# Weights read from PSUM, member matrices in pieces, pinned row fields and inputs prepared three tiles at a time in a four-layer graph network

## The chip, the cores and the metric

The kernel runs on one core of one Trainium2 chip. The time is device microseconds for one execution. Before the change the median of three runs is 3754.58 us (3746.37 to 3756.95). The engines are called TensorE (PE; its weight loads are shown apart as PEld), VectorE (DVE), ScalarE (ACT), GpSimd (POOL) and SyncE (SP). SP, ACT and POOL also issue DMA transfers. SBUF is the memory of the core that all engines read; PSUM is the small memory that TensorE writes.

## The reference

There are 1875 nodes with 256 values each, and 31875 edges sorted by destination, with 32 attributes, a type (0 to 7) and a weight each. Four layers follow each other; each has a graph part and a feed-forward part, and each part gets the normalised rows and is added to x.

- Layer 0: four rounds of GINE (for each edge relu(x[src] + edge_attr @ eW + eb), summed by destination, then two matrix products), and a feed-forward part on about half of the rows.
- Layer 1: attention over relations. For each edge the row of its source under the weights of its type, a score for each of 8 heads, a softmax over the edges of a destination, and the weighted sum. In short:

```
scores = leaky(h_src·attn_src + h_dst·attn_dst, 0.2)
amax   = max(segment_max(scores, dst), 0)
w      = exp(scores - amax[dst])
out    = segment_sum(h_src * w, dst) / (segment_sum(w, dst) + 1e-12)
```

  Then a feed-forward part of eight experts, one for each row, with a limit on rows.
- Layer 2: two GCN products (h = x @ W, then a sum over neighbours with dinv[src] * weight * dinv[dst], plus a bias; relu between them, softmax behind), then eight experts, two for each row, weighted.
- Layer 3: one GCN product with relu, added to its input, then sixteen experts, two for each row, and a final LayerNorm with gamma and beta.

## The kernel before

Rows are held in 15 tiles (NT) of 128 nodes, the last of 83; x stays in SBUF. A scheduler takes the program in its written order and may move instructions ahead on each engine; `later` keeps an instruction in program order. A tile pool gives each name a number of buffers, and a new use waits until the last reader of the old buffer is done. SP and ACT issue plain loads in the order of their own instructions; POOL issues indirect gathers and scatters.

**Attention** (fast_layer1_gnn, L835 and behind it). All rows under all eight relations, 264 values each (256 and the 8 source scores), lie in a table in DRAM. The edges of a destination tile are cut into 18 columns of 128 edges (12 for the last tile). For tile t `attention_edges` issues 18 gathers (L1122) into g, builds s16 (L873: 1 where the edge's destination is the column's node, 128 x 18 x 128) and sT (L879: its transpose, from a row of destinations), and computes the destination's score of every edge (L888, L890, L896). `attention_scores` forms the scores (L918) and runs a maximum within each column; `attention_weights` turns this into the maximum of each node (L950 through s16), brings it back to the edges (mk, L962 through sT), and stores exp of the score minus it into g's last 8 columns (L967). Three multiplications of six columns each (L970) weight the gathered rows in place. `attention_sums` adds up the edges by TensorE (L983) and divides (L985 to L988). The written order for each t is edges(t), scores(t-1), sums(t-2), weights(t-1). g has four buffers, s16 three, sT two, mk and ptop one each.

**GCN** (fast_gcn). Normalised tiles are transposed (L497) and copied to xT by ACT (L498), multiplied by W (L1019) and scaled into h (L1021); then for each tile 15 products with its adjacency tile (L1025) are summed and finished (L1028, L1030). The 15 adjacency tiles, 128 x 1920 float32 each, are loaded by SP (L997). In layers 2 and 3 all 15 tiles are normalised ahead, three at a time (`moments` with the square root on ACT, L1173, and L1205).

**Routing and experts.** Behind each group of finished tiles `route` picks two experts for each row, writes row, gate (L1772) and token number (L1773) into one of two row buffers, and scatters the rows to their slots (L1128). The two row buffers lie in one tile: in layer 2 in `first`, in layer 3 in a tile named rowbufs, of 2 * CH * 2 * (D + 2) values (CH is 3). `few_experts` then loads weights and slots for each block of rows, computes, and scatters the results to f_outs (L1128). When all are written (`complete`, a memset on POOL), the two outputs of each row are loaded (sum, L1912; even tiles on SP, odd ones on ACT, 15 buffers), added on POOL (L1913) and into x or y on DVE (L1914).

**The end** (layer3_ffn). Three tiles at a time: moments, L2009 and L2011, and the store.

Of the kernel before, what the change touches and what calls it, by code (L numbers as in the profile page):

```python
# [40 lines left out]
P = 128  # L41
N = 1875
NT = 15
# [56 lines left out]
class Net:  # L100
# [333 lines left out]
    def fast(self):  # L434
        with self.tc.tile_pool(name="win", bufs=1) as self.wpool:
# [5 lines left out]
            with self.tc.tile_pool(name="k2", bufs=1) as sb:  # L441
                r = self.router2(sb)
                self.fast_layer2_gnn(r)
                self.layer2_ffn(r)
            with self.tc.tile_pool(name="k3", bufs=1) as sb:
                r = self.router3(sb)
                self.fast_layer3_gnn(r)
                self.layer3_ffn(r)

    def slow(self):  # L450
# [9 lines left out]
        with self.tc.tile_pool(name="k2", bufs=1) as sb:  # L460
            r = self.router2(sb)
            self.route_all(self.route2, r)
            self.layer2_ffn(r)
        self.layer3_gnn()
# [397 lines left out]
    def attention_edges(self, t, table, ad3, hot, pools):  # L862
# [10 lines left out]
        nc.vector.tensor_tensor(s16, self.iota[:, None, :].to_broadcast([P, n, P]),  # L873
                                self.wdst[:, c0:c0 + n, None].to_broadcast([P, n, P]), ALU.is_equal)
# [4 lines left out]
        nc.vector.tensor_scalar(sT.rearrange("p j e -> p (j e)"), row, self.token[:, t:t + 1], None,  # L879
                                op0=ALU.is_equal)  # L880
# [61 lines left out]
    def attention_weights(self, a, pools):  # L942
# [24 lines left out]
        nc.scalar.activation(g[:, :, D:], sc, AF.Exp)  # L967
        for j0 in range(0, n, 6):
            v = g[:, j0:j0 + 6, :D].rearrange("p j (h d) -> p j h d", d=HD)
            nc.vector.tensor_tensor(v, v, g[:, j0:j0 + 6, D:, None].to_broadcast([P, 6, H, HD]),  # L970
                                    ALU.mult)
# [32 lines left out]
    def fast_gcn(self, pre, x, adj, wb, done):  # L1004
# [3 lines left out]
        with ExitStack() as ctx:  # L1008
# [5 lines left out]
            for t in range(NT):  # L1014
                xT = sb.tile([P, KD, P], F32, name="xT")
# [18 lines left out]
    def fast_layer2_gnn(self, r):  # L1034
        nc, tc, a = self.nc, self.tc, self.a
        with tc.tile_pool(name="q2a", bufs=1) as ap, tc.tile_pool(
            name="q2", bufs=1
        ) as one, tc.tile_pool(name="q2r", bufs=1) as rp:
# [5 lines left out]
            with tc.tile_pool(name="q2n", bufs=3) as sb:  # L1044
                self.layernorm_by(first, self.x, sb, CH)
# [16 lines left out]
            self.fast_gcn("d0", first, adj, ws[0], relu)  # L1062
            self.fast_gcn("d1", y, adj, ws[1], softmax)

    def fast_layer3_gnn(self, r):
        nc, tc, a = self.nc, self.tc, self.a
        with tc.tile_pool(name="q3a", bufs=1) as ap, tc.tile_pool(
            name="q3", bufs=1
        ) as one, tc.tile_pool(name="q3r", bufs=1) as rp:
# [3 lines left out]
            self.rows_in(r, one.tile([P, 1, ROWS], F32, name="rowbufs"))  # L1073
            with tc.tile_pool(name="q3n", bufs=3) as sb:
                for t in range(0, NT, CH):
                    self.layernorm(xl[:, t:t + CH, :], self.x[:, t:t + CH, :], sb)
                    for u in range(t, t + CH):
                        nc.gpsimd.tensor_tensor(self.x[:, u, :], self.x[:, u, :], xl[:, u, :],
                                                ALU.add)
# [7 lines left out]
            self.fast_gcn("d2", xl, adj, ws, add)  # L1087
# [119 lines left out]

    def layernorm_by(self, out, x, sb, n):

        for t in range(0, NT, n):  # L1210
            self.layernorm(out[:, t:t + n, :], x[:, t:t + n, :], sb)
# [507 lines left out]
    def route(self, r, ts, x, fill, weigh, sb, ps):  # L1719
# [37 lines left out]
        for i in range(2):  # L1757
# [10 lines left out]
            else:  # L1768
# [3 lines left out]
            nc.vector.tensor_copy(rows[:, :, i, D:D + 1], gates[i][:, :, None])  # L1772
            nc.vector.tensor_scalar(rows[:, :, i, D + 1:], self.token[:, sl, None], float(i * NP),  # L1773
                                    None, op0=ALU.add)
# [58 lines left out]
    def few_experts(self, pre, r, act, f, acc, w1n, w2n, b2n, affine):  # L1833
# [7 lines left out]
        with ExitStack() as ctx:  # L1841
# [63 lines left out]
            done = self.complete(g)  # L1905
            with tc.tile_pool(name=f"{pre}s", bufs=2) as sb:
                for t in range(NT):
                    n = min(P, N - t * P)
                    s = sb.tile([P, 2, D], F32, name="sum", bufs=NT)
                    v = r.outs[0:2 * NP, :].rearrange("(i n) d -> n i d", i=2)  # L1910
# [369 lines left out]
```

## Time and profile before

| | us |
|---|---|
| median of 3 runs | 3754.58 |
| profiled execution | 3750.91 |
| its span (first to last instruction) | 3749.1 |
| layer 0, GINE | about 100 to 1545 |
| layer-1 attention | 1860 to 2296 |
| layer-2 inputs | 2571 to 2610 |
| layer-2 GCN products | 2610 to 2860 |
| layer-2 experts | 2895 to 3235 |
| layer-3 inputs | 3235 to 3297 |
| layer-3 GCN product | 3297 to 3432 |
| layer-3 experts | 3432 to 3700 |
| end | 3700 to 3749 |

The granted TensorE clock is 0.888 on average. Over the span PE is busy 2895.0 us (77%), DVE 1891.3 (50%), POOL 1588.9 (42%), ACT 937.2 (25%).

A timeline row gives the start and the length of an instruction in us, its engine, its line in the kernel, what it writes and reads (out<-in), its shapes, and in brackets how long its engine stood idle before it and what ended that. SPq, ACTq and POOLq rows are the issuing of a DMA, not its transfer. A group row gives the count behind x, the busy time, the mean in ns of one, and the idle time before them.

### The profile page before, as it was taken

How to read it: one execution, taken by the hardware profiler on the slowest of the kernel's cores; microseconds unless marked ns; L12 is line 12 of the kernel's file. 1: busy time of each engine (PE TensorE's matmuls, PEld its weight loads, DVE VectorE, ACT ScalarE, POOL GpSimd, SP SyncE). 2: the span in 40 equal slices, each digit the busy share in tenths (PEclk: the TensorE clock that was granted, in tenths of full speed). 3: DMA queues.
4: the chain of work that ended last, by engine and by line, in shares of the span. 5: the costliest groups of instructions: out<-in, count | busy, mean ns of one | idle time of the engine just before them, and what ended most of it. 6: DMA issues, size and time to landing. Idle time of an engine off the chain costs nothing. (4 is left out here: it accounts for less than half of the span.)

```text
span 3749.1 us, 43548 instructions
## 1 busy us (share of the span) xinstructions
PE 2895.0 (77%) x14049; PEld 2402.2 (64%) x14049; DVE 1891.3 (50%) x5527; ACT 937.2 (25%) x2026; POOL 1588.9 (42%) x1603
## 2 busy tenths in 40 slices
PE   3878789979997999668735555884986999596994
PEld 2667678768776877446524444663875888475773
DVE  5566577756675676683246663016145111445334
ACT  1333233323332333213311111110133222122221
POOL 2777477757775777100177771001011111313222
PEclk9999899989998999789967666896987999798997
DMA  5434656655664453113444430524002555513664
GB/s 147 124 110 129 198 152 202 184 155 162 185 186 136 132 122 113 48 38 96 144 120 142 143 106 29 164 86 173 1 18 80 193 179 177 197 71 96 206 202 136
DMA packets 330707, 495.36 MB, mean 132 GB/s; under 512 B 79601, under 2 KB 258724, under 8 KB 328676
## 3 DMA queue, kind: packets, MB, share of 16 engines
q1 hardware_dynamic: 250804, 286.21, 24.3%
q0 software_dynamic: 72672, 199.68, 18.1%
q10 hardware_dynamic: 6992, 6.58, 0.5%
q8 instruction: 113, 1.85, 0.2%
q14 instruction: 126, 1.03, 0.1%
HBM read 369.90 MB, written 122.43 MB: 131 GB/s over the span
## 5 line engine op out<-in xcount | busy, mean ns | idle before, releaser
L1122 POOL DMA_INDIRECT g<-qt,w_src x1056 | 1036.8, 982 | 431.0 <-issue 351.7
L623 PE MATMUL acc<-m,s 128*128 128x256 f32 (+1 forms) x2112 | 560.6, 389 | 15.5 <-ACT m L610 15.5
L594 PE MATMUL pe<-ew,w_attr 128*128 128x256 f32 x1888 | 509.1, 395 | 69.2 <-DVE g L609 68.6
L609 DVE TENSOR_TENSOR g<-g,pe 128x512 f32<-128x512 f32 x528 | 360.2, 682 | 398.1 <-DMA g<-qt,w_src 341.0
L610 ACT ACTIVATE m<-g 128x512 f32<-128x512 f32 x528 | 332.7, 631 | 795.3 <-DVE g L609 610.0
L1122 POOL DMA_INDIRECT g<-rq_h,w_tsrc x264 | 304.6, 1154 | 390.8 <-PE pz L888 311.0
L594 PEld LDWEIGHTS pe<-ew,w_attr 128*128 128x128 f32 x1888 | 364.2, 197 | 153.4 <-DVE g L609 88.0
L623 PEld LDWEIGHTS acc<-m,s 128*128 128x128 f32 x2112 | 404.8, 196 | 65.0 <-ACT m L610 17.0
L1893 PE MATMUL hid<-xeT,w 128*128 128x256 f32 x1184 | 271.6, 386 | 23.5 <-DVE xeT L1888 23.5
L1899 PE MATMUL out<-w,hidT 128*128 128x256 f32 x1184 | 264.0, 379 | 0.0
L1893 PEld LDWEIGHTS hid<-xeT,w 128*128 128x128 f32 x1184 | 221.1, 192 | 62.6 <-DVE xeT L1888 30.8
L1895 ACT ACTIVATE hidT<-hid,cols 128x256 f32<-128x256 f32 x296 | 138.5, 474 | 450.3 <-PE hid L1893 434.0
L1899 PEld LDWEIGHTS out<-w,hidT 128*128 128x128 f32 x1184 | 225.0, 190 | 30.6
L601 DVE TENSOR_TENSOR s<-iota,w_dst 128x256 f32<-128x256 f32 x528 | 219.3, 416 | 0.0
L401 PE MATMUL padj<-col,row 128*128 128x240 f32 x720 | 207.3, 383 | 15.1 <-DVE col L374 13.0
L1902 DVE TENSOR_TENSOR ye<-out,b 128x256 f32<-128x256 f32 x104 | 44.1, 424 | 313.3 <-PE out L1899 313.3
L1128 POOL DMA_INDIRECT f_outs<-ye,f2place x44 | 42.7, 971 | 299.8 <-DVE ye L1903 276.2
L401 PEld LDWEIGHTS padj<-col,row 128*128 128x128 f32 x720 | 141.7, 199 | 37.2 <-DVE col L374 9.9
L1128 POOL DMA_INDIRECT f_slots<-first,slot x30 | 29.6, 988 | 286.4 <-issue 206.7
L374 DVE TENSOR_SCALAR col<-wide,g_col,g_wt 128x240 f32<-128x240 f32 x360 | 146.4, 407 | 0.0
L983 PE MATMUL acc<-g,s 128*128 128x264 f32 x528 | 139.4, 422 | 5.5 <-issue 3.0
L1128 POOL DMA_INDIRECT f_outs<-ye,f3place x60 | 57.7, 961 | 201.6 <-DVE ye L1903 198.8
(425 smaller groups left out, 4330.0 us busy)
## 6 DMA issues: line engine op xcount, KB each, us to landing
f_slots<-zeros SPq DMA_DIRECT2D x45, 1032.0 KB
w<-in_L_ffn_W SPq DMA_DIRECT2D x44, 1024.0 KB
adj<-adj SPq DMA_DIRECT2D x45, 960.0 KB
w<-in_L_ffn_w SPq DMA_DIRECT2D x60, 512.0 KB
w<-in_L_ffn_w SPq DMA_DIRECT2D x18, 1024.0 KB
g<-qt,w_src POOLq DMA_INDIRECT x1056
dstrow<-lin SPq DMA_DIRECT2D x14, 1152.0 KB
rq_h<-hr SPq DMA_DIRECT2D x8, 1980.0 KB
```

Source lines behind the costliest of these rows:

```text
L374: pin(nc.vector.tensor_scalar(col, self.wide, self.gcol[:, i:i + 1], self.gwt[:, i:i + 1], op0=ALU.is_equal, op1=ALU.mult))
L401: pin(nc.tensor.matmul(pa[:, u // GT, :], row, col, start=u % GT == 0, stop=u % GT == GT - 1))
L594: pin(nc.tensor.matmul(pes[q][:, v, :], at[:, v, :], self.ew[:, i, :], start=True, stop=True))
L601: pin(nc.vector.tensor_tensor(ss[q], self.iota[:, None, :].to_broadcast([P, 2, P]), self.wdst[:, c:c + 2, None].to_broadcast([P, 2, P]), A ...
L609: pin(nc.vector.tensor_tensor(g, g, pes.pop(q), ALU.add))
L610: pin(nc.scalar.activation(m[:, :, :D], g, AF.Relu))
L623: pin(nc.tensor.matmul(accs[t], s[:, v, :], m[:, v, :], start=k == v == 0, stop=end and v == 1))
L983: nc.tensor.matmul(acc, s[:, j, :], g[:, j, :], start=j == 0, stop=j == n - 1)
L1122: self.nc.gpsimd.indirect_dma_start(out=out, out_offset=None, in_=table, in_offset=bass.IndirectOffsetOnAxis(ap=at, axis=0))
L1893: nc.tensor.matmul(p1, w1[:, kc, m * P:(m + 1) * P], xT[:, kc, :], start=kc == 0, stop=kc == KD - 1)
L1895: nc.scalar.activation(hT[:, m, :], p1, act, bias=v[:, m:m + 1])
L1899: nc.tensor.matmul(p2, hT[:, m, i * P:(i + 1) * P], w2[:, m, :], start=m == 0, stop=m == fc - 1)
```

## The change

Five things change together.

1. In the attention ACT copies the softmax weights into PSUM (into mk, whose values are used by then), and the multiplications read them from there; s16 and sT are each written in pieces of six columns.
2. `fast_gcn` takes a function `ready` that prepares three tiles; it is called for the first six tiles ahead of the first transpose, and then three tiles ahead. Layer 2 gives the LayerNorm.
3. `few_experts` no longer loads and adds the outputs. `outputs_of` does so for one tile. For layer 2's experts it is called in layer 3's `ready`, which takes six pieces of rowbufs in place of the 15 sum buffers; the adjacency loads come ahead of it in the program.
4. In the last stage `outputs_of` is called for three tiles ahead of their LayerNorm, with 9 sum buffers.
5. The writes of gate and token number keep their place in program order.

```diff
@@ fast
+            r2 = r
             with self.tc.tile_pool(name="k3", bufs=1) as sb:
                 r = self.router3(sb)
-                self.fast_layer3_gnn(r)
+                self.fast_layer3_gnn(r, r2)
@@ attention_edges
-        nc.vector.tensor_tensor(s16, self.iota[:, None, :].to_broadcast([P, n, P]),
-                                self.wdst[:, c0:c0 + n, None].to_broadcast([P, n, P]), ALU.is_equal)
+        for j in range(0, n, 6):
+            nc.vector.tensor_tensor(s16[:, j:j + 6], self.iota[:, None, :].to_broadcast([P, 6, P]),
+                                    self.wdst[:, c0 + j:c0 + j + 6, None].to_broadcast([P, 6, P]),
+                                    ALU.is_equal)
...
-        nc.vector.tensor_scalar(sT.rearrange("p j e -> p (j e)"), row, self.token[:, t:t + 1], None,
-                                op0=ALU.is_equal)
+        for j in range(0, n, 6):
+            nc.vector.tensor_scalar(sT[:, j:j + 6].rearrange("p j e -> p (j e)"),
+                                    row[:, j * P:(j + 6) * P], self.token[:, t:t + 1], None,
+                                    op0=ALU.is_equal)
@@ attention_weights
+        weights = mk[:, :, 0, :]
+        nc.scalar.copy(weights, g[:, :, D:])
         for j0 in range(0, n, 6):
             v = g[:, j0:j0 + 6, :D].rearrange("p j (h d) -> p j h d", d=HD)
-            nc.vector.tensor_tensor(v, v, g[:, j0:j0 + 6, D:, None].to_broadcast([P, 6, H, HD]),
-                                    ALU.mult)
+            nc.vector.tensor_tensor(v, v, weights[:, j0:j0 + 6, :, None]
+                                    .to_broadcast([P, 6, H, HD]), ALU.mult)
@@ fast_gcn
             for t in range(NT):
+                if ready and t % CH == 0:
+                    for u in (0, CH) if t == 0 else (t + CH,):
+                        if u < NT:
+                            ready(range(u, u + CH))
                 xT = sb.tile([P, KD, P], F32, name="xT")
@@ fast_layer2_gnn
-            with tc.tile_pool(name="q2n", bufs=3) as sb:
-                self.layernorm_by(first, self.x, sb, CH)
+            def ready(ts):
+                sl = slice(ts[0], ts[-1] + 1)
+                self.layernorm(first[:, sl, :], self.x[:, sl, :], np2)
...
-            self.fast_gcn("d0", first, adj, ws[0], relu)
+            self.fast_gcn("d0", first, adj, ws[0], relu, ready)
@@ fast_layer3_gnn
-            self.rows_in(r, one.tile([P, 1, ROWS], F32, name="rowbufs"))
-            with tc.tile_pool(name="q3n", bufs=3) as sb:
-                for t in range(0, NT, CH):
-                    self.layernorm(xl[:, t:t + CH, :], self.x[:, t:t + CH, :], sb)
-                    for u in range(t, t + CH):
-                        nc.gpsimd.tensor_tensor(self.x[:, u, :], self.x[:, u, :], xl[:, u, :],
-                                                ALU.add)
+            buf = one.tile([P, 1, ROWS], F32, name="rowbufs")
+            self.rows_in(r, buf)
+            room = [buf[:, 0, i * 2 * D:(i + 1) * 2 * D].rearrange("p (i d) -> p i d", i=2)
+                    for i in range(ROWS // (2 * D))]
+
+            def ready(ts):
+                for t in ts:
+                    self.outputs_of(r2, t, room[t % len(room)], self.x)
+                sl = slice(ts[0], ts[-1] + 1)
+                self.layernorm(xl[:, sl, :], self.x[:, sl, :], np3)
+                for t in ts:
+                    nc.gpsimd.tensor_tensor(self.x[:, t, :], self.x[:, t, :], xl[:, t, :], ALU.add)
...
-            self.fast_gcn("d2", xl, adj, ws, add)
+            self.fast_gcn("d2", xl, adj, ws, add, ready)
@@ route
-            nc.vector.tensor_copy(rows[:, :, i, D:D + 1], gates[i][:, :, None])
-            nc.vector.tensor_scalar(rows[:, :, i, D + 1:], self.token[:, sl, None], float(i * NP),
-                                    None, op0=ALU.add)
+            self.later(nc.vector.tensor_copy(rows[:, :, i, D:D + 1], gates[i][:, :, None]))
+            self.later(nc.vector.tensor_scalar(rows[:, :, i, D + 1:], self.token[:, sl, None],
+                                               float(i * NP), None, op0=ALU.add))
@@ few_experts
-            done = self.complete(g)
-            with tc.tile_pool(name=f"{pre}s", bufs=2) as sb:
-                for t in range(NT):
-                    n = min(P, N - t * P)
-                    s = sb.tile([P, 2, D], F32, name="sum", bufs=NT)
-                    v = r.outs[0:2 * NP, :].rearrange("(i n) d -> n i d", i=2)
-                    queue = nc.scalar if t % 2 else nc.sync
-                    self.behind(queue.dma_start(s[:n], v[t * P:t * P + n]), done)
-                    nc.gpsimd.tensor_tensor(s[:n, 0, :], s[:n, 0, :], s[:n, 1, :], ALU.add)
-                    nc.vector.tensor_tensor(acc[:n, t, :], acc[:n, t, :], s[:n, 0, :], ALU.add)
+            r.done = self.complete(g)
+
+    def outputs_of(self, r, t, s, acc):
+
+        nc = self.nc
+        n = min(P, N - t * P)
+        v = r.outs[0:2 * NP, :].rearrange("(i n) d -> n i d", i=2)
+        queue = nc.scalar if t % 2 else nc.sync
+        self.behind(queue.dma_start(s[:n], v[t * P:t * P + n]), r.done)
+        nc.gpsimd.tensor_tensor(s[:n, 0, :], s[:n, 0, :], s[:n, 1, :], ALU.add)
+        nc.vector.tensor_tensor(acc[:n, t, :], acc[:n, t, :], s[:n, 0, :], ALU.add)
@@ layer3_ffn
             for t in range(0, NT, CH):
                 ts = slice(t, t + CH)
+                for u in range(t, t + CH):
+                    self.outputs_of(r, u, sb.tile([P, 2, D], F32, name="sum", bufs=9), y)
```

More of the change, by code (lines that the diff above doesn't have):

```diff
@@ L463, in slow @@
             self.layer2_ffn(r)
+            with self.tc.tile_pool(name="k2s", bufs=4) as sp:
+                for t in range(NT):
+                    self.outputs_of(r, t, sp.tile([P, 2, D], F32, name="sum"), self.x)
         self.layer3_gnn()
@@ L1002, in gcn_weights, with fast_gcn @@
         return self.weight(sb, w, f"gw{i}"), self.vector_row(sb, b, f"gb{i}")
-    def fast_gcn(self, pre, x, adj, wb, done):
+    def fast_gcn(self, pre, x, adj, wb, done, ready=None):
         nc, tc = self.nc, self.tc
@@ L1037, in fast_layer2_gnn @@
             name="q2", bufs=1
-        ) as one, tc.tile_pool(name="q2r", bufs=1) as rp:
+        ) as one, tc.tile_pool(name="q2r", bufs=1) as rp, tc.tile_pool(name="q2n", bufs=3) as np2:
             ws = [self.gcn_weights(one, i, a[f"L2_gnn_W{i}"], a[f"L2_gnn_b{i}"]) for i in (1, 2)]
@@ L1060, in softmax, with fast_layer3_gnn @@
                 self.route_behind(self.route2, r, t, rp, ps)
-            self.fast_gcn("d0", first, adj, ws[0], relu)
+            self.fast_gcn("d0", first, adj, ws[0], relu, ready)
             self.fast_gcn("d1", y, adj, ws[1], softmax)
-    def fast_layer3_gnn(self, r):
+    def fast_layer3_gnn(self, r, r2):
         nc, tc, a = self.nc, self.tc, self.a
@@ L1068, in fast_layer3_gnn @@
             name="q3", bufs=1
-        ) as one, tc.tile_pool(name="q3r", bufs=1) as rp:
+        ) as one, tc.tile_pool(name="q3r", bufs=1) as rp, tc.tile_pool(name="q3n", bufs=2) as np3:
             ws = self.gcn_weights(one, 3, a["L3_gnn_W"], a["L3_gnn_b"])
@@ L1206, in layernorm @@
                                          op0=ALU.subtract, op1=ALU.mult)
-    def layernorm_by(self, out, x, sb, n):
-        for t in range(0, NT, n):
-            self.layernorm(out[:, t:t + n, :], x[:, t:t + n, :], sb)
     def affine(self, x, g, b):
@@ L1831, in routed, with few_experts @@
         return filled
-    def few_experts(self, pre, r, act, f, acc, w1n, w2n, b2n, affine):
+    def few_experts(self, pre, r, act, f, w1n, w2n, b2n, affine):
         nc, tc, a = self.nc, self.tc, self.a
@@ L1961, in layer2_ffn @@
     def layer2_ffn(self, r):
-        self.few_experts("e2", r, AF.Gelu, 4 * D, self.x, "L2_ffn_W1", "L2_ffn_W2", "L2_ffn_b2",
-                         True)
+        self.few_experts("e2", r, AF.Gelu, 4 * D, "L2_ffn_W1", "L2_ffn_W2", "L2_ffn_b2", True)
     def router3(self, sb):
@@ L2000, in layer3_ffn @@
                 nc.gpsimd.tensor_tensor(self.x[:, t, :], self.x[:, t, :], bet, ALU.add)
-            self.few_experts("e3", r, AF.Relu, 2 * D, y, "L3_ffn_w1", "L3_ffn_w2", "L3_ffn_b2",
-                             False)
+            self.few_experts("e3", r, AF.Relu, 2 * D, "L3_ffn_w1", "L3_ffn_w2", "L3_ffn_b2", False)
             for t in range(0, NT, CH):
                 ts = slice(t, t + CH)
+                for u in range(t, t + CH):
+                    self.outputs_of(r, u, sb.tile([P, 2, D], F32, name="sum", bufs=9), y)
                 v = y[:, ts, :]
```

## The prediction

> **What bounds the kernel now.** I read the page first. Over the whole span TensorE is busiest (77%), but the change touches stages that other things bound, so I cut the span into stretches, and read each with its groups and its timeline. Time in the first fence is start:end, length, then the busy time of PE, PEld, DVE, ACT and POOL, granted clock, DMA share and GB/s.
>
> ```profile
> 1860.00:2296.00 436.00, 224.15 (x1878) 180.99 (x1878) 260.84 (x472) 68.06 (x176) 300.81 (x261) 0.69 0.40 115
> 2571.00:2610.00 39.00, 29.02 (x130) 23.95 (x131) 18.48 (x73) 6.03 (x19) 0.07 (x1) 0.79 0.92 374
> 3235.00:3297.00 62.00, 24.19 (x113) 19.61 (x114) 36.79 (x105) 7.20 (x21) 23.95 (x32) 0.66 0.78 301
> ```
>
> The attention (first row) is bound by POOL's gathers: busy 301 of 436 us, and between two of them lie only about 0.30 us of "issue". So what counts there is how long one gather takes.
>
> ```profile
> L609 DVE TENSOR_TENSOR g<-g,pe 128x512 f32<-128x512 f32 x528 | 360.2, 682 | 398.1 <-DMA g<-qt,w_src 341.0
> L1122 POOL DMA_INDIRECT g<-rq_h,w_tsrc x264 | 304.6, 1154 | 390.8 <-PE pz L888 311.0
> L970 DVE TENSOR_TENSOR g<-g 128x1536 f32<-128x1536 f32 x44 | 74.7, 1750 | 1.1 <-ACT g L967 1.1
> L873 DVE TENSOR_TENSOR s<-iota,w_dst 128x2304 bf16<-128x2304 f32 (+1 forms) x15 | 37.4, 2496 | 0.0
> L879 DVE TENSOR_SCALAR sT<-dstrow,token 128x2304 bf16<-128x2304 f32 (+1 forms) x15 | 20.9, 1391 | 0.0
> ```
>
> The mean gather is 1154 ns, but one alone takes 0.95 to 0.96. The timeline (start, us) shows where the rest is lost:
>
> ```profile
> 2067.82 0.95 POOL L1122 DMA_INDIRECT g<-rq_h,w_tsrc  x1 [0.30 <-issue]
> 2068.72 2.55 DVE L873 TENSOR_TENSOR s<-iota,w_dst 128x2304 bf16<-128x2304 f32 x1
> 2069.08 3.02 POOL L1122 DMA_INDIRECT g<-rq_h,w_tsrc  x1 [0.30 <-issue]
> 2073.66 1.84 POOL L1122 DMA_INDIRECT g<-rq_h,w_tsrc  x1 [0.31 <-issue]
> 2073.98 1.41 DVE L879 TENSOR_SCALAR sT<-dstrow,token 128x2304 bf16<-128x2304 f32 x1
> 2076.04 5.08 DVE L970 TENSOR_TENSOR g<-g 128x1536 f32<-128x1536 f32 x3
> 2077.07 1.54 POOL L1122 DMA_INDIRECT g<-rq_h,w_tsrc  x1 [0.30 <-issue]
> 2078.92 1.36 POOL L1122 DMA_INDIRECT g<-rq_h,w_tsrc  x1 [0.30 <-issue]
> ```
>
> A gather that starts inside one of three DVE instructions ends some 0.83 us after that instruction does (2068.72 + 2.55 = 2071.27; the gather ends at 2072.10). All three read SBUF only. Adding what each gather takes above 0.957 gives 52.4 us: 20.6 beside s16 (L873), 11.3 beside sT (L879), 20.4 beside the multiply (L970).
>
> In the layer-3 stretch the order of the loads decides:
>
> ```profile
> 3235.00 8.16 SPq L1912 DMA_DIRECT2D sum<-f_outs  x8
> 3255.73 20.35 SPq L997 DMA_DIRECT2D adj<-adj  x15
> 3273.47 0.65 ACT L498 COPY xT<-mm 128x256 f32<-128x256 f32 x2 [4.35 <-DVE xl L1205]
> ```
>
> The expert outputs are loaded and added first, and only then the 15 adjacency tiles. The first xT copy stands at 3273.47, the last h (L1021) ends at 3296.4, and GCN sums follow.
>
> **A, attention.** (1) The multiply takes its weights from PSUM. Does that free the gathers? L609 in layer 0 has just this form (one operand SBUF, one PSUM): 102 gathers beside nothing but it average 955 ns, 9 beside L890 (PSUM too) 955. So I take the 20.4 us as gone; bounds 0 and 20.4. The multiply's length stays (682 ns for 512 elements and 1750 for 1536 lie on one slope). (2) s16 and sT in pieces of 768: about 0.95 and 0.77 us each, by their slopes over size. A gather comes every 0.957 + 0.305 = 1.262 us; if it meets an instruction of length L at random it loses on average L - 0.63 where L is longer than this cycle, L²/2.52 where shorter. sT now: 0.78 a tile by that, 0.77 measured; s16 now: 1.92, 1.40 measured. In pieces: s16 3 x 0.36 = 1.08 (0.79 if scaled as measured), sT 3 x 0.23 = 0.70. Over 14.67 full tiles 22 to 26 us stay, so 28 of 52.4 go. Bounds: 0 (neither the PSUM operand nor the pieces help) and 42. DVE's extra 17 us (per tile 0.3 + 0.9) are hidden: it is busy 261 of 436. (3) 15 ACT copies, 0.31 us as L967's exp, join the chain exp, copy, multiply; ACT is at 16%, and in the middle POOL's gathers hide them. (4) The order shifts on PE: the maximum matmuls of tile t-1 (L950) now stand behind the sums of tile t-2 (L983, 10.0 us). Behind the last gather I count 35.7 us to the end of the last sum, from 33.8 now: +2 (-3 to +5). A = -28 + 2 = -26 (-45 to +5).
>
> [...]
>
> **B, layer-2 inputs.** ACT runs five square roots ahead of all xT copies; the first copy is at 2581.64, though the second square root is at 2570.61. In the new order two square roots, then copies, so the first copy can come near 2572.3; PE then goes on at 1.365 us a tile (as 2586.4 to 2603.4 now). But the later chunks' normalisation holds it in part. h ends near 2597 instead of 2605.5: -8 (-12 to 0). Adjacency loads, 2571.5 to 2608, do not bind: a sum needs only its own tile.
>
> **C, layer-3 inputs.** The adjacency loads no longer wait for the sum buffers, so SP issues them at about 3235, ahead of its 8 loads of expert outputs. The 15 tiles of 960 KB run at 421 GB/s, 2.33 us each, 35 us together, and the last of 15 issues came 20.35 us after the first because each waits for the one 8 before it. So the first output load goes out near 3256 and, behind seven tiles in SP's queue, lands near 3272 (now 3237). On ACT the 7 loads share semaphores with those tiles: the first waits to about 3258, the last for a free slot of six, whose POOL adds (0.84 each) begin at 3273: near 3282. ACT's table load (1.28) and square roots stand behind all seven. First xT copy about 3287 instead of 3273.5: +14. If output loads were not held behind the tiles, the adjacency would be early and h would end near 3288: -8. With the third round of six slots a further 6 late: +20. The POOL adds into x are not needed before the first sum. C = +14 (-8 to +20).
>
> [...]
>
> **D, pinned rows.** L1773 was run ahead and then stood in DVE's queue until a scatter had left its buffer. In most groups PE covers that. At the end of layer 3 it does not:
>
> ```profile
> 3409.13 0.15 DVE L1773 TENSOR_SCALAR rowbufs<-token 128x1 f32<-128x1 f32 x1 [1.59 <-DMA f_slots<-rowbufs,slot]
> 3414.74 0.15 DVE L1773 TENSOR_SCALAR rowbufs<-token 128x1 f32<-128x1 f32 x1 [3.68 <-DMA f_slots<-rowbufs,slot]
> ```
>
> With L1028 and the router's chain behind it, 1.6 + 3.7 = 5.3 are to be had; pinned writes go behind their slot and put 0.3 into that chain, and layer 2's end adds nothing I could see. D = -4 (-6 to 0).
>
> **E, the end.** Sum buffers fall from 15 to 9, so ACT's last load stands behind one square root; POOL's adds (0.84 each) pace this, 3704 to 3720. 0 (-2 to +3).
>
> Sum: -26 - 8 + 14 - 4 + 0 = -24. The profiled execution took 3750.91 (span 3749.1, 1.8 around it), 3.7 below the median shown. So 3727 on its basis, 3731 against the median. A change under 0.3% (11 us) cannot be told from none.
>
> **The rivals** (times against the median). *Layer 3 not delayed*: C = -8, 3709. For it: the odd tiles have a queue of their own; against: ACT waits for the tiles' semaphores anyway. *All stalls go*: gathers slip between pieces as between the three multiplies (1.36 against 1.75 of DVE), A = -40, 3717. Against: three gathers in a row lost 0.4 to 0.6 there. *PSUM does not free the gathers*, and the pieces only spread what is lost: A = +2, 3759. Against: the 955 ns. *The chain of a tile becomes the bound*, slower than before: scores, maximum, mk, exp, copy, multiply, 10.0 us of sums and then L950 follow each other on DVE, ACT and PE. I count 23.0 us from one tile's gathers to the next turn, against 22.7 for 18 gathers without stalls and 25.5 (382.7/15) now. It decides above 25.5. At 26.5 the stage loses 15 instead of gaining 26: -8 + 14 - 4 + 15 = +17, 3772. For it: the moved L950 and one PSUM buffer for mk held until the multiply; against: DVE idles 9 us before a tile's scores (L918, at 2225.74).
>
> **How the numbers follow.** Chances: forecast 0.53, layer 3 not delayed 0.10, all stalls go 0.10, PSUM no help 0.14, chain bound 0.13. The first three are faster (0.73), PSUM no help is within 0.3% (0.14), the chain is slower (0.13). The range 3703 to 3759 leaves out the chain and a little of the low end.
>
> **What would show it.** A: L1122's mean near 1.04 us (957 + 24/264), gathers beside nothing but the multiply near 955, and the last gather starting near 2210; wrong if gathers beside the multiply exceed 1.3 us, or if POOL idles for g buffers released by L983. B: the first xT copy near 2572 relative to the same start. C: the adjacency issued before the outputs, and the first xT copy some 53 us after the memset that closes the experts (3234.2) instead of 39. D: no wait of DVE on a scatter at the end of layer 3. The forecast fails most easily where the six slots and ACT's queue behave otherwise than worked out in C, or where A's tile chain runs past its gathers.

## The result and the profile after

The changed kernel takes 3686.18 us (median of 4 runs, 3684.54 to 3687.9), the kernel before beside it 3754.26 (4 runs): ratio 0.9822, 95% interval 0.9805 to 0.9839. The forecast was faster, 3731, with a range from 3703 to 3759. The direction was right and the size was not: 68 us gained, where 24 were predicted.

The two profiled executions (spans 3749.1 and 3685.5 us) were cut at the same events. All times are in us:

| stretch | before | after | difference | predicted |
|---|---|---|---|---|
| start to the first gather of the attention | 1855.3 | 1858.2 | +3.0 | 0 |
| A: first gather to the last addition into x | 420.7 | 387.5 | -33.2 | -26 |
| B: from there to the last h of layer 2's first product | 329.6 | 319.6 | -10.0 | -8 |
| D: second product of layer 2, first to last L1028 | 137.6 | 104.1 | -33.5 | 0 |
| from there to the end of the last layer-2 expert scatter | 371.1 | 373.2 | +2.1 | 0 |
| C: from there to the last h of layer 3 | 63.8 | 88.2 | +24.4 | +14 |
| D: product of layer 3, first to last L1028 | 116.4 | 102.2 | -14.1 | -4 |
| from there to the last expert scatter of layer 3 | 283.4 | 286.0 | +2.6 | 0 |
| E: from there to the end | 50.5 | 45.6 | -4.9 | 0 |

(The 118.5 us from the last h of layer 2's first product to the second's first L1028, and the 2.5 us between layer 3's last h and its first L1028, are the same in both.) So 47.6 of the 63.6 us lie in the two stretches of D, which the prediction had priced at 4. (The two D rows count from the start of the first such addition to the end of the last; the line is L1028 in the kernel before, L1043 in the changed one.)

Three of the stretches, as windows of the changed kernel: the attention, the second product of layer 2, and the inputs of layer 3 (start:end, length, busy time of PE, PEld, DVE, ACT and POOL, granted clock, DMA share, GB/s):

```profile
1860.00:2266.00 406.00, 231.20 (x1936) 185.17 (x1933) 264.43 (x522) 75.47 (x191) 268.30 (x263) 0.71 0.43 125
2683.80:2787.90 104.10, 101.46 (x508) 87.63 (x506) 69.97 (x359) 49.10 (x94) 21.09 (x21) 1.00 0.07 26
3163.00:3250.00 87.00, 26.42 (x113) 21.19 (x114) 32.04 (x106) 7.30 (x21) 23.19 (x34) 0.62 0.57 214
```

The second row's stretch in the kernel before, which the prediction did not show:

```profile
2724.00:2861.60 137.60, 115.08 (x508) 99.74 (x506) 69.25 (x360) 50.83 (x95) 23.75 (x24) 0.86 0.10 33
```

TensorE has the same 508 matmuls in both. Before it is busy 115 of 138 us at a granted clock of 0.86, after 101 of 104 at 1.00: 20 us of idle time are gone, and the same matmuls take 14 us less.

In the attention the gathers still bind. From the page of the changed kernel, and a part of its timeline:

```profile
L1144 POOL DMA_INDIRECT g<-rq_h,w_tsrc x264 | 269.7, 1022 | 390.5 <-PE pz L896 311.0
```

```profile
2033.12 0.96 POOL L1144 DMA_INDIRECT g<-rq_h,w_tsrc  x1 [0.30 <-issue]
2033.14 5.08 DVE L981 TENSOR_TENSOR g<-g,mk 128x1536 f32<-128x1536 f32 x3
2034.38 0.96 POOL L1144 DMA_INDIRECT g<-rq_h,w_tsrc  x1 [0.30 <-issue]
2035.64 0.96 POOL L1144 DMA_INDIRECT g<-rq_h,w_tsrc  x1 [0.30 <-issue]
2036.90 0.95 POOL L1144 DMA_INDIRECT g<-rq_h,w_tsrc  x1 [0.30 <-issue]
2039.41 0.95 DVE L878 TENSOR_TENSOR s<-iota,w_dst 128x768 bf16<-128x768 f32 x1
2039.42 1.77 POOL L1144 DMA_INDIRECT g<-rq_h,w_tsrc  x1 [0.30 <-issue]
```

The mean gather fell from 1154 to 1022 ns. Four gathers beside the multiply with its weights in PSUM take 0.95 to 0.96; one that starts together with a piece of s16 still takes 1.77.

Layer 3's inputs, from the timeline of the changed kernel (the memset that closes the experts starts at 3162.66):

```profile
3162.78 17.34 ACTq L1930 DMA_DIRECT2D rowbufs<-f_outs  x7
3164.02 30.35 SPq L1008 DMA_DIRECT2D adj<-adj  x15
3194.47 21.37 SPq L1930 DMA_DIRECT2D rowbufs<-f_outs  x8
3208.75 2.45 POOL L1931 TENSOR_TENSOR rowbufs<-rowbufs 128x256 f32<-128x256 f32 x3 [16.46 <-DMA rowbufs<-f_outs]
3219.63 0.74 ACT L502 COPY xT<-mm 128x256 f32<-128x256 f32 x2 [5.44 <-PE mm L501]
3225.97 0.99 DVE L1932 TENSOR_TENSOR x<-x,rowbufs 83x256 f32<-83x256 f32 x1 [3.76 <-POOL rowbufs L1931]
3228.40 1.22 PE L1040 MATMUL acc<-xl,adj 128*128 128x256 f32 x2 [4.61 <-DVE xl L1036]
```

SP issues 15 adjacency tiles and only then its 8 output loads (the even tiles), whose first data reach POOL at 3208.75, 46 us behind the memset. On DVE the addition of the last tile stands ahead of the first h, so TensorE waits once more.

The experiments ran in four groups, each with its own runs of the kernel before: (1) pins_only, sums_in_layer2, outputs_first and psum_only; (2) psum_only_b, pieces_only, sums_in_layer2_b and outputs_first_b; (3) token_pin, outputs_on_act, layer2_ahead and end_as_before; (4) ln_pool_open and att_both. In the first and the third of them every kernel, before included (4149.89 and 4192.4 us), took about 400 us more; totals are compared within a group only, and the attention of those groups is read apart, in the last section.

### The profile page after: what moved, and what is told of

Same layout as the page of the kernel before. It is cut to its first block, busy times and chain, and to the rows that moved or that the text cites. A ratio compares the mean times of both kernels' runs of the same rounds, so it can differ in the third digit from the quotient of the medians.

```text
span 3685.5 us, 43628 instructions
## 1 busy us (share of the span) xinstructions
PE 2883.6 (78%) x14049; PEld 2393.4 (65%) x14049; DVE 1889.1 (51%) x5585; ACT 945.2 (26%) x2041; POOL 1553.9 (42%) x1603
## 5 line engine op out<-in xcount | busy, mean ns | idle before, releaser
L627 PEld LDWEIGHTS acc<-m,s 128*128 128x128 f32 x2112 | 404.7, 196 | 65.3 <-ACT m L614 17.4
L1144 POOL DMA_INDIRECT g<-rq_h,w_tsrc x264 | 269.7, 1022 | 390.5 <-PE pz L896 311.0
```

The costliest lines, as they stand in the source:

```text
L627: pin(nc.tensor.matmul(accs[t], s[:, v, :], m[:, v, :], start=k == v == 0, stop=end and v == 1))
L1144: self.nc.gpsimd.indirect_dma_start(out=out, out_offset=None, in_=table, in_offset=bass.IndirectOffsetOnAxis(ap=at, axis=0))
```

## The experiments

What the traces of the runs show, by the stretches above (us; A in brackets where the group was one of the two just named):

| run | A | B | D, layer 2 | C | D, layer 3 | E |
|---|---|---|---|---|---|---|
| before | 420.7 | 329.6 | 137.6 | 63.8 | 116.4 | 50.5 |
| after | 387.5 | 319.6 | 104.1 | 88.2 | 102.2 | 45.6 |
| pins_only | (464.7) | 329.7 | 104.1 | 64.1 | 102.2 | 50.1 |
| token_pin | (478.2) | 329.8 | 104.3 | 64.3 | 102.2 | 50.5 |
| psum_only | (506.5) | 329.7 | 137.7 | 65.4 | 116.8 | 50.3 |
| psum_only_b | 407.1 | 329.5 | 137.8 | 64.2 | 117.2 | 50.0 |
| pieces_only | 406.0 | 327.6 | 137.4 | 64.1 | 117.1 | 50.4 |
| att_both | 387.4 | 329.7 | 134.1 | 64.8 | 117.3 | 50.4 |
| sums_in_layer2 | (536.8) | 319.6 | 104.0 | 52.5 | 102.2 | 46.5 |
| sums_in_layer2_b | 379.7 | 319.5 | 104.0 | 53.2 | 102.2 | 46.2 |
| outputs_first | (530.9) | 319.4 | 104.1 | 49.9 | 102.2 | 45.3 |
| outputs_first_b | 384.0 | 319.5 | 104.1 | 48.8 | 102.2 | 46.3 |
| outputs_on_act | (550.6) | 319.1 | 104.1 | 72.0 | 102.2 | 45.6 |
| layer2_ahead | (551.0) | 320.6 | 104.1 | 90.7 | 102.2 | 46.5 |
| end_as_before | (550.2) | 319.7 | 104.1 | 89.1 | 102.2 | 50.4 |
| ln_pool_open | 421.3 | 320.3 | 134.0 | 64.2 | 116.2 | 50.3 |

### The pinned writes: pins_only and token_pin

pins_only is the kernel before with the change's last part alone; token_pin pins only the second of the two writes:

```diff
-            nc.vector.tensor_scalar(rows[:, :, i, D + 1:], self.token[:, sl, None], float(i * NP),
-                                    None, op0=ALU.add)
+            self.later(nc.vector.tensor_scalar(rows[:, :, i, D + 1:], self.token[:, sl, None],
+                                               float(i * NP), None, op0=ALU.add))
```

> The kernel before with only the gate and token writes (L1772, L1773) kept in program order. Theory: in the kernel before, the token write stood early in DVE's queue and waited for the scatters of the group two before, about 3 us each time; the softmax, the LayerNorm and the router stood behind it, TensorE ran out of work for about 5 us in each group and its granted clock fell to about 0.8 for the next matmuls. Then this edit alone takes the second GCN product of layer 2 (first to last L1028) from 137.6 to about 104 us and that of layer 3 from 116.4 to about 102, some 46 us in all: 3708 us, ratio 0.988. Rival, the prediction's step D: only the waits at the end of layer 3 are on the path, 4 us: 3750 us; then the 34 us of layer 2 came from another part.

> The kernel before with only the token write (L1773) kept in program order, the gate write (L1772) left free. Theory: it is the token write that was run ahead of its group and waited for the scatters of the group two before, so this alone brings the whole gain of pinning both: second GCN product of layer 2 (first to last L1028) near 104 us in place of 137.6, layer 3 near 102 in place of 116.4, about 3705 us where before takes 3752. Rival: then the gate write is run ahead in its place and waits as long; little gain, above 3740.

pins_only: 4100.76 against 4149.89, ratio 0.9893 (0.9838 to 0.9948). token_pin: 4147.23 against 4192.4, ratio 0.9904 (0.987 to 0.9938). In both the two products take what they take in the changed kernel, 104 and 102 us; psum_only, in the first group too but without pins, has 138 and 117. The theory holds in both places, and pinning the token write alone is enough. (Two kernels without pins, att_both and ln_pool_open, have 134 us in layer 2 where the other unpinned ones have 137 to 138; why stays open.) The waits of the kernel before in the two products (total us, times, longest), and then of the changed kernel:

```profile
DVE first L1773 <- DMA f_slots<-first,slot: 28.1, 8, 6.5
...
PE mm L497 <- DVE rxl L1936: 15.6, 3, 5.7
...
DVE rowbufs L1773 <- DMA f_slots<-rowbufs,slot: 28.3, 8, 4.7
```

```profile
PE mm L501 <- DVE rxl L1954: 2.2, 3, 0.8
```

How 28 us of waiting on DVE reach TensorE is seen in one group of the kernel before:

```profile
2746.97 5.43 PE L1025 MATMUL acc<-y,adj 128*128 128x256 f32 x24
...
2760.90 0.17 DVE L1773 TENSOR_SCALAR first<-token 128x3 f32<-128x3 f32 x1 [3.19 <-DMA f_slots<-first,slot]
2764.66 0.17 DVE L1773 TENSOR_SCALAR first<-token 128x3 f32<-128x3 f32 x1 [2.75 <-DMA f_slots<-first,slot]
...
2770.80 1.09 PE L497 MATMUL mm<-ident,rxl 128*128 128x128 f32 x4 [5.44 <-DVE rxl L1936]
2771.68 1.06 PE L1025 MATMUL acc<-y,adj 128*128 128x256 f32 x2
...
2777.84 7.58 PE L1025 MATMUL acc<-y,adj 128*128 128x256 f32 x24
```

and in the same place of the changed kernel:

```profile
2725.76 0.73 PE L501 MATMUL mm<-ident,rxl 128*128 128x128 f32 x4 [0.61 <-DVE rxl L1954]
2726.33 0.60 PE L1040 MATMUL acc<-y,adj 128*128 128x256 f32 x2
...
2729.56 5.43 PE L1040 MATMUL acc<-y,adj 128*128 128x256 f32 x24
```

DVE starts nothing else while the token write waits (3.19 and 2.75 us), and behind it stand the softmax of the next tile and the LayerNorm that the group's transposes (mm) need. On TensorE the sums of the next tiles stand behind those transposes. So TensorE stands idle for 5.44 us, and 24 matmuls, which took 5.43 us before, take 7.58 afterwards. From one group's transposes to the next it is 33.3 us before (2770.80 to 2804.10), 23.0 after (2725.76 to 2748.73). The granted clock, 0.86 in this stretch and 1.00 in the changed kernel, says why:

```profile
2768.60:2782.20 13.60, 11.40 (x36) 9.82 (x37) 8.24 (x51) 5.58 (x12) 0.00 (x0) 0.50 0.00 0
```

The clock falls from 1.00 to 0.50 at 2768.56, 3.2 us into the idle stretch, and is back at 2782.21; 317 ns a matmul in this window stand against 204 in the 23 us ahead of it. It is the same at the next two stretches, of 5.71 and 4.43 us: half clock from 4.3 and 3.0 us into them, for 10.2 us each. Behind the idle stretches of 0.6 to 0.8 us in the changed kernel the clock stays at 1.00. In layer 3's product of the kernel before, 3.4 us at half clock also follow an idle stretch of 2.77 us, and none follow one of 2.46 us. What decides when the clock falls was not shown.

### The attention: psum_only, psum_only_b, pieces_only, att_both

psum_only (and psum_only_b, the same kernel) is the kernel before with the ACT copy and the multiply from PSUM; pieces_only has s16 and sT in pieces; att_both has both and nothing else.

```diff
+        weights = mk[:, :, 0, :]
+        nc.scalar.copy(weights, g[:, :, D:])
...
-            nc.vector.tensor_tensor(v, v, g[:, j0:j0 + 6, D:, None].to_broadcast([P, 6, H, HD]),
-                                    ALU.mult)
+            nc.vector.tensor_tensor(v, v, weights[:, j0:j0 + 6, :, None]
+                                    .to_broadcast([P, 6, H, HD]), ALU.mult)
```

> The kernel before with only the softmax weights read from PSUM (with the ACT copy); s16 and sT stay whole. Theory: a multiply with one operand in PSUM does not hold up the gathers, so the 20.4 us above 0.957 beside the multiply go and the 32 us beside s16 and sT stay: gathers mean about 1080 ns, last gather 20 us earlier, 3754 - 20 = 3734 us, ratio 0.995. Rival: what counts is the length of DVE's instructions, and the pieces bring the gain: last gather within 5 us of before, 3750 us.

> The same kernel as psum_only. On the chip of that run all kernels took some 400 us more than shown for before and after (before 4150): TensorE stood idle for 'issue' between its matmuls (91 us at L623 alone) while gathers ran, and in the attention the chain of a tile was the bound, with POOL idle for 4 to 10 us a tile. Theory: on a chip where before takes about 3755 the gathers bind, and this edit gives 3734. Rival: the deeper order that the PSUM copy brings (L950 behind the sums of two tiles before) makes the chain the bound there too, 3755 to 3780.

> The kernel before with only s16 and sT written in pieces of six columns; the weights stay in SBUF. Theory of the prediction: the pieces leave most of the loss beside s16 and sT (22 to 26 of 32 us), so 6 to 10 us go, and the 20 beside the multiply stay: 3746 us where before takes 3755. Rival, by the trace of the changed kernel (13.3 us left beside s16 and sT together): pieces alone take 18 to 19, 3736.

> The kernel before with the attention of the changed kernel and nothing else. Theory: the two edits hinder each other's stalls, and together leave some 15 us above 0.957 in the gathers; from the first gather to the last addition into x 387 us in place of 420.7 (alone 407.1 and 406.0): 33 us, time about 3719 where before takes 3752. Rival: they add up, 28 us, 392 us; the other 5 us of the changed kernel came from elsewhere.

psum_only itself came out slower than before in its group (4188.69 against 4149.89, ratio 1.01, 1.0066 to 1.0134), which neither its theory nor its rival gave; the last section takes that up. psum_only_b: 3738.42 against 3751.77, ratio 0.9968 (0.9956 to 0.9981); the theory gave 3734. pieces_only: 3737.95, ratio 0.9967 (0.9952 to 0.9981). att_both: 3719.32 against 3755.62, ratio 0.9902 (0.9886 to 0.9919). What the gathers take above 0.957 us, put down to that one of s16, sT and the multiply that each overlaps most (us; "others" overlap none of them):

| | beside s16 | beside sT | beside the multiply | others | all |
|---|---|---|---|---|---|
| before | 20.6 | 11.3 | 20.4 | 0.2 | 52.4 |
| psum_only_b | 22.8 | 11.6 | 0 | 0.3 | 34.7 |
| pieces_only | 6.9 | 7.1 | 23.8 | 0.3 | 38.1 |
| att_both | 12.4 | 3.1 | 0.9 | 0.6 | 17.0 |
| after | 12.9 | 3.1 | 0.9 | 0.5 | 17.4 |

From the timeline of psum_only_b:

```profile
2012.69 5.07 DVE L973 TENSOR_TENSOR g<-g,mk 128x1536 f32<-128x1536 f32 x3
2013.28 0.95 POOL L1125 DMA_INDIRECT g<-rq_h,w_tsrc  x1 [0.30 <-issue]
2014.53 0.95 POOL L1125 DMA_INDIRECT g<-rq_h,w_tsrc  x1 [0.30 <-issue]
...
2040.41 2.52 DVE L873 TENSOR_TENSOR s<-iota,w_dst 128x2304 bf16<-128x2304 f32 x1
2040.54 3.22 POOL L1125 DMA_INDIRECT g<-rq_h,w_tsrc  x1 [0.30 <-issue]
```

Beside the multiply nothing is lost any more, beside the whole s16 as much as ever. So the PSUM operand does what it was taken to do (the last gather ends 18 us earlier), but alone it gives back 5 us behind the last gather (40.7 to the last addition, before 35.9), and 13.5 are left. The pieces alone take 14.7, more than the 6 to 10 predicted and less than the 18 to 19 of the rival. Both together take 33.2, more than the sum of 28: of the 5 us between, 2.7 lie behind the last gather (38.0 in place of 40.7), the others in the gathers, where the pieces alone had put more of the loss beside the multiply (23.8 in place of 20.4). The theory of att_both holds; the rival (plain addition) falls. Where gathers and pieces happen to meet still moves A: sums_in_layer2_b and outputs_first_b have the same attention code, lose 10.0 and 14.2 us in the gathers in place of 17.0, and A is 379.7 and 384.0 us.

### Layer 3's inputs: sums_in_layer2, outputs_first, outputs_on_act

sums_in_layer2 (and sums_in_layer2_b) takes back the moved additions alone; the LayerNorm stays three tiles at a time:

```diff
         self.few_experts("e2", r, AF.Gelu, 4 * D, "L2_ffn_W1", "L2_ffn_W2", "L2_ffn_b2", True)
+        with self.tc.tile_pool(name="e2s", bufs=2) as sb:
+            for t in range(NT):
+                self.outputs_of(r, t, sb.tile([P, 2, D], F32, name="sum", bufs=NT), self.x)
@@ fast_layer3_gnn, ready
-                for t in ts:
-                    self.outputs_of(r2, t, room[t % len(room)], self.x)
```

outputs_first and outputs_first_b split outputs_of into its load and its additions, and load all tiles ahead of the adjacency:

```diff
-            adj = self.adjacency_tiles(ap)
             xl = one.tile([P, NT, D], F32, name="xl")
...
+            room = [xl[:, i:i + 2, :] for i in (0, 2)] + room
+            room += [r.y[:, i:i + 2, :] for i in range(0, NT - 1, 2)]
+            for t in range(NT):
+                self.load_outputs(r2, t, room[t])
+            adj = self.adjacency_tiles(ap)
...
-                    self.outputs_of(r2, t, room[t % len(room)], self.x)
+                    self.add_outputs(t, room[t], self.x)
```

(The lines are those of outputs_first_b. outputs_first has two pieces at the end of xl for the last two tiles instead; there the LayerNorm of earlier tiles overwrites them, so what is added for those two tiles is not what was loaded.) In all four runs each output tile also has room of its own in place of the six shared pieces. outputs_on_act leaves the changed kernel's order and pieces and takes all output loads, those at the end too, to ACT's queue:

```diff
-        queue = nc.scalar if t % 2 else nc.sync
+        queue = nc.scalar
```

> The changed kernel, but the outputs of layer 2's experts are loaded into 15 buffers and added at the end of layer 2, as in the kernel before; layer 3's adjacency loads come behind them again, and only the LayerNorm is prepared three tiles at a time. Theory: of the changed kernel's layer-3 inputs 24 us are lost by loading the adjacency first, so this takes last h of layer 3 from 86.6 us behind the memset that closes the experts to about 62 (before: 62.2) or somewhat less, since the LayerNorm is no longer all ahead of the first copy: 3686 - 24 to -30, 3656 to 3662 us. Rival: the slower stage comes from the order on DVE and ACT that ready brings, not from the loads: then it stays near 3686.

> The changed kernel, but in layer 3 all 15 loads of expert outputs are issued ahead of the adjacency loads, each into room of its own (6 pieces of rowbufs, 7 of the still unused output tile, 2 of xl's end); the additions stay three tiles at a time. Theory: what cost 24 us is the place of the output loads behind 15 adjacency tiles in SP's queue; ahead of them they land within about 9 us, the adjacency by about 46 us behind the memset, and the last h, then bound by PE's 1.365 us a tile from about 12 us on, near 35 to 45 us behind the memset in place of 86.6: 3686 - 42 to -52, about 3640 us. Rival: the loads of outputs and adjacency share the 421 GB/s whatever the order, and POOL's additions pace the stage: last h 60 to 70, 3660 to 3670 us.

> The same kernel as sums_in_layer2, where the last h of layer 3 came 52.5 us behind the last expert scatter in place of 88.2 (changed kernel) and 63.8 (before), but the attention was slower on that chip. Theory: where before takes 3755, 36 us below the changed kernel: about 3650. Rival: 3686, if the gain in the layer-3 inputs is given back in the layer behind it.

> The changed kernel with all 15 output loads ahead of the adjacency loads, each in room of its own: two pieces of xl for the first two tiles, six of rowbufs, seven of the unused output tile. Theory: the last h comes 45 to 50 us behind the last expert scatter (88.2 in the changed kernel): 38 to 43 us below it, about 3645 where before takes 3755. Rival: as sums_in_layer2, 36 below, since POOL's additions pace both.

> The changed kernel with all 15 output loads of outputs_of on ACT's queue instead of every second one; the adjacency loads stay ahead in SP's queue, the six pieces of rowbufs and 9 sum buffers stay. Theory: what is slow in the changed kernel is that 8 output loads stand behind 15 adjacency tiles in the same queue; in a queue of its own a load is served beside them (the odd tiles landed about every 5 us), so the first three tiles are in by about 15 us behind the memset, the first xT copy comes some 20 to 30 us earlier than its 57 us, and the last h near 65 to 75 us behind the last expert scatter in place of 88.2: 13 to 23 us less time. Rival: the six pieces, each free only after POOL's and DVE's additions, and the bytes shared with the adjacency pace the stage: last h stays above 82, time within 6 us.

sums_in_layer2_b: 3631.08 against 3751.77, ratio 0.9675 (0.9659 to 0.9691), the fastest kernel of this study. outputs_first_b: 3642.52, ratio 0.9711 (0.9693 to 0.9729). In the first group sums_in_layer2 took 4143.42 against 4149.89 (0.9994, 0.9973 to 1.0015) and outputs_first 4138.57 (0.9967, 0.9938 to 0.9996); outputs_on_act, in the third, 4193.07 against 4192.4 (1.0002, 0.9974 to 1.0029), where layer2_ahead and end_as_before, with the changed kernel's order of loads, took 4210.3 and 4207.44.

The last h comes 53 (sums_in_layer2_b; 52.5 in sums_in_layer2) and 49 us (outputs_first_b; 49.9 in outputs_first) behind the last expert scatter instead of 88. That is some 10 us better than the theory of sums_in_layer2 had it (about 62, counted from the memset), a little worse than that of outputs_first (35 to 45) and as that of outputs_first_b had it (45 to 50). From the timeline of sums_in_layer2_b:

```profile
3146.77 8.31 SPq L1925 DMA_DIRECT2D sum<-f_outs  x8
...
3168.47 21.01 SPq L1005 DMA_DIRECT2D adj<-adj  x15
3172.85 0.80 ACT L499 COPY xT<-mm 128x256 f32<-128x256 f32 x2 [2.99 <-PE mm L498]
```

The adjacency is issued 22 us later than the outputs, and the first xT copy stands 26 us behind SP's first output load, where the changed kernel has it 57 us behind the memset. So the place of the loads and their six pieces together cost 35 us, and the rest of the change in this stretch by itself gains 11 (53 against 63.8). Of the 51 us between the spans of the changed kernel (3685.5) and sums_in_layer2_b (3634.2), 35 lie here; most of the others, 7.8 each, lie ahead of the attention and in it, where kernels with the same code differ by as much; with them the time fell 19 us below the 3650 that the theory of sums_in_layer2_b gave. From the timeline of outputs_on_act (the memset is at 3678.28):

```profile
3678.40 8.15 ACTq L1930 DMA_DIRECT2D rowbufs<-f_outs  x8
...
3702.45 0.74 ACT L502 COPY xT<-mm 128x256 f32<-128x256 f32 x2 [2.13 <-PE mm L501]
...
3731.66 0.72 POOL L1931 TENSOR_TENSOR rowbufs<-rowbufs 83x256 f32<-83x256 f32 x1 [13.45 <-DMA rowbufs<-f_outs]
...
3736.50 0.80 ACT L502 COPY xT<-mm 128x256 f32<-128x256 f32 x2 [16.49 <-PE mm L501]
```

With a queue of their own the first eight loads are issued within 8 us and the first xT copy stands 24 us behind the memset, although the adjacency still stands ahead of them in the program. The stretch falls by 16 us, within what the theory gave. The last tiles still come late (3731.66), so 72.0 us stay where 53 are possible. The last load is issued by 3704.5, so what holds that tile for another 27 us is not the wait for a piece; that its data share the bandwidth with the adjacency is the author's guess, and was not tested apart. The first data of a load from ACT's queue reach POOL 3 us behind the memset, here (3681.23) and in the changed kernel (3165.66); the first of a load behind the tiles in SP's queue 46 us behind it.

### Layer 2's inputs: layer2_ahead and ln_pool_open

The change also opens the pool of layer 2's LayerNorm (q2n, `np2`) for the whole of fast_layer2_gnn, in a line that the diff above leaves out; before, it was closed ahead of the product. layer2_ahead takes ready away from layer 2's first product, with the pool left where the change put it. ln_pool_open is the kernel before with that pool alone:

```diff
-        ) as one, tc.tile_pool(name="q2r", bufs=1) as rp:
+        ) as one, tc.tile_pool(name="q2r", bufs=1) as rp, tc.tile_pool(name="q2n", bufs=3) as np2:
...
-            with tc.tile_pool(name="q2n", bufs=3) as sb:
-                self.layernorm_by(first, self.x, sb, CH)
+            self.layernorm_by(first, self.x, np2, CH)
```

> The changed kernel with layer 2's inputs normalised all ahead again (ready is not passed to its first GCN product). Theory: ready there took 10 us, since the first xT copies no longer stand behind five square roots; the last h of that product comes 10 us later after the attention's end: 3696 us where the changed kernel takes 3686. Rival: the 10 us come from the scheduler's other choices behind the attention, and stay: 3686.

> The kernel before, with only the pool of layer 2's LayerNorm (q2n) opened for the whole of fast_layer2_gnn instead of being closed ahead of the GCN product. Theory: closed, its room goes to the xT buffers of the product, and the first xT copy waits until the LayerNorm has read its last small tile; kept open, the copies start with the first tiles, and the last h of layer 2's first product comes 9 to 10 us earlier: from the attention's end 320 us in place of 329.6, the time 9 to 10 us below before. Rival: the removal of five square roots ahead of the copies in program order is what counts, and ready is one of several ways to it: 329 us, the time as before.

layer2_ahead: 4210.3 against 4192.4, ratio 1.0063 (1.0032 to 1.0093); stretch B 320.6. So the preparation three tiles at a time is worth 1 us here, and the theory of 10 us fell. ln_pool_open: 3746.91 against 3755.62, ratio 0.9978 (0.9968 to 0.9989); B 320.3, and from its timeline:

```profile
2570.40 0.20 ACT L1172 ACTIVATE rs_sd<-ln_ve 128x3 f32<-128x3 f32 x1 [1.45 <-DVE f2seen L1694]
2571.99 0.80 ACT L498 COPY xT<-mm 128x256 f32<-128x256 f32 x2 [1.38 <-PE mm L497]
```

The copy stands behind two square roots without any ready (before it stood behind five, at 2581.64). Keeping the pool open is enough for 9.3 of the 10 us. That the closed pool's room is handed to the product's buffers, and that the wait comes from there, fits this (in the kernel before, the first copy's wait at 2581.64 is put down to DVE's last LayerNorm instruction, L1205, which ends at 2581.54) and was not shown apart.

### The end: end_as_before

```diff
+            for u in range(NT):
+                self.outputs_of(r, u, sb.tile([P, 2, D], F32, name="sum", bufs=NT), y)
             for t in range(0, NT, CH):
                 ts = slice(t, t + CH)
-                for u in range(t, t + CH):
-                    self.outputs_of(r, u, sb.tile([P, 2, D], F32, name="sum", bufs=9), y)
```

> The changed kernel with the last outputs loaded and added for all 15 tiles ahead of the final LayerNorm, into 15 buffers, as before. Theory: the change there took 5 us (from the last expert scatter to the end 45.6 us, 50.5 before), because DVE does the LayerNorm of early tiles while it waits for the sums of the later ones; undone, the end grows to 50.5 and the time by 5 us. Rival, the prediction's step E: nothing hangs on it, 45 to 46 us either way.

4207.44 against 4192.4, ratio 1.0051 (1.0022 to 1.008); the end takes 50.4 again. The change there is worth 5 us. (The changed kernel itself did not run in this group, so the stretch says this and the total does not.) DVE waits 12.3 us for the sums there before the change and 7.6 after it.

## Why the prediction was right or wrong

- **A was right in mechanism and within its bounds** (-33.2; -26 given, -45 to +5). The multiply's 20.4 went. The mis-sized term is the pieces: 22 to 26 us were to stay in the gathers, 17.4 did. A piece of sT takes 0.60 to 0.61 us and not 0.77: the slope over size overstated a short instruction. The rest is the assumption that gathers meet pieces at random; what is lost beside s16 alone varies from 5.9 to 12.9 us between kernels with the same attention code.
- **B had the right size by luck, with the wrong cause.** "ACT runs five square roots ahead of all xT copies" was read rightly; that ready would undo it was not. The pool's life did (ln_pool_open).
- **C had the right sign, and the size was past its bound** (+24.4; +14 given, -8 to +20). The even tiles do stand behind the adjacency, which was the author's estimate and had no run behind it, but landed 46 us behind the memset, not 38: the issue of the 15 adjacency tiles took 30.35 us in place of the 20.35 that the prediction carried over, while the odd tiles were loaded beside them. On ACT the prediction was wrong: the odd tiles were not held behind the adjacency (near 3258 to 3282 in its times, 24 to 48 us behind the memset) but were issued within 17 us. And it missed that the last tile's addition stands on DVE ahead of the first h (3.76 us of wait, 4.61 on TensorE).
- **D was the step that failed**: "In most groups PE covers that", and "layer 2's end adds nothing I could see". The trace of before shows 28 us of such waits in each product. The prediction looked at the two at the end of layer 3 and took the others as covered, without reading what TensorE itself waits for in that stretch: 15.6 us for rxl in three waits, a fourth of 9.1 us at the stretch's end, and a clock of 0.86. The price also lacked the clock: 0.50 behind three idle stretches of 4.4 to 5.7 us, 317 ns a matmul behind the first in place of 204 ahead of it. Measured: 47.6 us, 33.5 of them in layer 2, and pins_only has both stretches as the changed kernel has them.
- **E** was 5 us, not 0, outside its bounds (-2 to +3): the LayerNorm of early tiles now fills part of DVE's wait for the sums of late ones.
- With 47.6 in place of 4 for D the sum would have been -68 us; the two profiled spans differ by 63.6, the medians by 68. That it comes so near is luck: A, B and E gained 14 us more than forecast, C gained 10 us less, and the stretches that were not to change lost 8.
- The rivals: the time lies beyond all of them, since each let D stand at 4 us. In the attention, where 33.2 were gained, "all stalls go" (40) was as near as the forecast (26). The rival by which the PSUM operand frees nothing fell: beside the multiply the loss went from 20.4 us to 0 in psum_only_b. There a gather takes 0.95 us beside L973, which reads one operand from PSUM, and 3.22 beside the whole s16, whose inputs are both in SBUF.

## What to carry to other kernels

A wait on an engine that is half idle can cost what stands behind it in its queue, and then behind that on the next engine (here 28.1 us on DVE, busy 69 of 138 us, and 15.6 us on TensorE); before calling it covered, list what the bounding engine itself waits for in exactly that stretch, not its share of a longer one. Small stores that a scheduler may run ahead (here a token number into a row buffer still being sent) are worth pinning (0.9893 of before in pins_only, 0.9904 in token_pin). A load that the next step needs at once should not stand behind bulk loads in the same queue (first data 46 us behind the memset there, 3 us in ACT's queue): giving the place of the loads and their buffers back took the time from 0.982 to 0.968 of before, with 35 of the 51 us in that stage.

## What the runs showed of the hardware

In the two groups in which the kernel before took 4150 and 4192 us, TensorE stood idle for "issue" between matmuls while gathers ran. From the page of psum_only (in the profile before it is 15.5 us idle, all of it waiting for ACT):

```profile
L623 PE MATMUL acc<-m,s 128*128 128x256 f32 (+1 forms) x2112 | 622.9, 415 | 94.4 <-issue 91.4
```

The line belongs to layer 0, and some 350 of the 400 us lie ahead of the attention: it starts at 2196 to 2221 us in these groups, at 1855 in the profile before. The changed attention took 531 to 551 us and the one of before 465 to 478, and psum_only was slower than before (1.01). The gathers beside its multiply are as fast as elsewhere (nothing is lost there above 0.957), but POOL stands idle 3 to 10 us between tiles. So POOL's gathers no longer bind alone; that the chain of a tile became longer than they are, as the slower rival of the prediction has it, would fit, but the profile puts most of POOL's idle time down to "issue", so it is not shown. Behind the attention the stretches are as in the other groups (104 and 102 us for the two products). What made TensorE's issue slow was not settled; the first and the second group ran on a chip of the same number, so the chip, which the expectation of psum_only_b names, does not explain it by itself.
